# Layer 3 as one pass over x3 with a tap lead of five row groups; layer 2's token factor kept on chip

## The chip, the cores and the metric

The kernel runs on one core of a Trainium2 chip. The metric is device time in microseconds for one execution. The kernel before takes 3590.95 us (median of three runs, 3589.71 to 3592.86). A profile of one execution gives the start and length of every instruction on TensorE (PE), VectorE (DVE), ScalarE (ACT), GpSimd (POOL) and SyncE (SP, which here only issues DMAs).

## The reference, cut to what matters

The input x is a 256 x 256 image with 128 channels, in fp32. Four layers each add something to it, after a group norm over groups of four channels (`_gn`): attention with a triangle bias, a triangle product of 16 channels, a triangle product of 128 channels (layer 2), and a stack of small convolutions (layer 3). The change touches layers 2 and 3.

```python
# layer 2, on z = _gn(x)
zn = layernorm(z)                               # a mean and a root per token
a = sigmoid(zn @ Wga + bga) * (zn @ Wla + bla)
b = sigmoid(zn @ Wgb + bgb) * (zn @ Wlb + blb)
k = einsum('bimc,bmjc->bijc', a, b)
out = sigmoid(zn @ Wgo + bgo) * (layernorm(k) @ Wlo + blo)

# layer 3, on x = _gn(x); c1 is a 1 x 9 convolution with one output channel,
# c2 a product over channels at each token
t = relu(c1(x))
y = concat([x[:, :1], x[:, 1:] + t[:, :-1]], axis=1)
u = relu(c1(y))
z = u + roll(y, 1, axis=1)                      # the last two rows differ
v = relu(c2(z))
p = concat([z[:, :, :1], z[:, :, 1:] + v[:, :, :-1]], axis=2)
r = relu(c2(p))
q = r + roll(p, 1, axis=2)                      # the last two columns differ
```

In layer 3 t and u have a single channel: they are images of 256 x 256 numbers. Since y differs from x by an image that is the same in all channels, c1(y) is c1(x) plus a nine-tap filter of t with the channel sums of the weights, moved down by one row.

## The kernel before, in words

Activations lie in DRAM transposed, 128 channels by 65,536 tokens (`x2T`, `x3T` and others). A stage works through 32 tiles of 2048 tokens (`SC`), a tile of [128 channels, 2048] being eight rows of the image. Every DMA of the stages named here is issued by SP, in program order. The stages with `tc.manual_schedule()` keep the written order on each engine.

*Layer 2, gated products* (L833 to L957, names `p5_...`). Blocks of four tiles. `sums5` forms each token's mean and mean square with matmuls on 32-column strips, `compact5` stores the block's variance to DRAM and reads it back as [128, 64], `root5` and `factor5` take root and reciprocal of that small tile and store it, and `spread5` reads it back broadcast over 128 partitions into the tile `p5_zn`. `normalise5` then multiplies in place, in one DVE instruction of 2048 elements per tile. `product5` makes a gate or a linear product of 1024 tokens (two matmuls) into one of three PSUM buffers; ACT takes the sigmoid of the gate, DVE multiplies the linear product in. The results are stored to `aD` and `bD`, token row first: [128, channel, 512].

*Layer 2, triangle product* (L958 to L1018). Four channels per step are loaded from `aD` and `bD`, transposed and multiplied; K goes to `kD`. *Layer 2, end* (L1022 to L1079) normalises k and z with `broadcast_rows` (L819): four matmuls that spread rows of factors over 128 partitions into two PSUM tiles. For z it uses the tile `rs2`, which POOL loads from DRAM.

*Layer 3, tap pass* (L1115 to L1127). All of x3 is read; one matmul per 512 tokens gives the nine tap sums, which POOL's queue stores to `sD`. *Layer 3, image stage* (L1130 to L1189). The whole images t and u are formed once, and moved by rows through DRAM (`imgD`). Their sum e is added to all channels later. *Layer 3, main loop* (L1196 to L1309, `p9_...`). x3 is read again in groups of eight rows, each tile with the row above it. Per group: ACT scales x into z and q; `finish_z` adds e, spread by `broadcast_rows`, on DVE; `p_half` and `q_half` each run half of a c2 product, with DVE taking relu and sum from PSUM; POOL's `residual` adds p into q; `emit` transposes a finished group back on PE, and ACT copies it out. Two product tiles (`psM`) and two further tiles (`psX`: broadcast and transposes in turn) fill the PSUM.

Of the kernel before, what the change touches and what calls it, by code (L numbers as in the profile page):

```python
# [31 lines left out]
def kernel(ctx: ExitStack, tc: tile.TileContext, a: dict, out: bass.AP):  # L32
# [19 lines left out]

    aD = dram.tile([P, D, 2 * N], F32, name="aD")
    bD = dram.tile([P, D, 2 * N], F32, name="bD")
    vrD = dram.tile([1, T], F32, name="vrD")
    rs2D = dram.tile([1, T], F32, name="rs2D")
# [3 lines left out]
    sD = dram.tile([32, T], F32, name="sD")  # L60
    imgD = dram.tile([4, T], F32, name="imgD")
# [81 lines left out]
    b2 = column("L3_conv_b2")  # L143

# [52 lines left out]
    with tc.tile_pool(name="x0", bufs=1) as xres, tc.tile_pool(name="p0", bufs=3) as sb:  # L197
# [18 lines left out]
        with tc.tile_pool(name="f0", bufs=1) as fsb, tc.tile_pool(name="f0ps", bufs=1, space=PSUM) as ps:  # L216
# [29 lines left out]
            pb2 = ps.tile([P, 6], F32, name="f0_pb2")  # L246
# [4 lines left out]
            nc.vector.tensor_tensor(b2w, b2w, pb2, ALU.add)  # L251
            pt_ = ps.tile([P, NH], F32, name="f0_pt")
# [103 lines left out]
    with tc.tile_pool(name="p2c", bufs=1) as cs:  # L356
# [39 lines left out]
        with tc.tile_pool(name="p2", bufs=2) as sb, tc.tile_pool(name="p2e", bufs=6) as eb, tc.tile_pool(  # L396
# [159 lines left out]
            for j in range(2 * NG + 5):  # L556
# [5 lines left out]
                if not 0 <= out[0] < NG:  # L562
                    out = None
                if half == 0 and nxt:
                    tiles(nxt)
# [266 lines left out]

    rs2_pool = ctx.enter_context(tc.tile_pool(name="rs2", bufs=1))  # L833
    KB = 4
    BT = KB * SC
    with tc.tile_pool(name="p5", bufs=2) as sb, tc.tile_pool(name="p5psX", bufs=1, space=PSUM) as psX, tc.tile_pool(
        name="p5psM", bufs=3, space=PSUM
# [13 lines left out]
        def store_block(dram_row, b, t):  # L851

            by_c = dram_row.rearrange("o (s c t) -> c (o s) t", c=4, t=CK)
            for c in range(4):
                nc.sync.dma_start(
                    by_c[c, b * KB : (b + 1) * KB, :], t[32 * c + b * KB : 32 * c + (b + 1) * KB, :]
                )

        def sums5(b):
            st = psX.tile([P, 2, CK], F32, name="p5_st")  # L860
# [13 lines left out]
            return var  # L874

        def compact5(b, var):
            store_block(vrD, b, var)
            vars_[b] = sb.tile([P, BT // P], F32, name="p5_vc")
            nc.sync.dma_start(
                vars_[b], vrD[:, b * BT : (b + 1) * BT].rearrange("o (p t) -> p (o t)", p=P)  # L880
            )

        def root5(v):
            nc.vector.tensor_scalar(v, v, 0.0, None, ALU.max)
            nc.scalar.activation(v, v, AF.Sqrt, bias=epst)

        def factor5(b):
            v = vars_.pop(b)
            nc.vector.reciprocal(v, v)
            nc.sync.dma_start(  # L890
                rs2D[:, b * BT : (b + 1) * BT].rearrange("o (p t) -> p (o t)", p=P), v
            )

        def spread5(s):
            if s < NSC:
                zns[s] = sb.tile([P, SC], F32, name="p5_zn", bufs=3)
                nc.sync.dma_start(zns[s], rs2D[:, s * SC : (s + 1) * SC].to_broadcast([P, SC]))

        def normalise5(s):
            if s < NSC:  # L900
                nc.vector.scalar_tensor_tensor(zns[s], xs[s], m2, zns[s], ALU.subtract, ALU.mult)  # L901
                del xs[s]
# [14 lines left out]
        var = sums5(0)  # L917
        root5(var)
        fac = sb.tile([P, CK], F32, name="p5_fac", bufs=1)
        nc.vector.reciprocal(fac, var)  # L920
        store_block(rs2D, 0, fac)
        for s in range(2):
            spread5(s)
        normalise5(0)
        for s in range(NSC):
# [5 lines left out]
            for h in range(2):  # L931
                hs = slice(h * H2, (h + 1) * H2)
                for i in range(2):
                    pg = product5(s, 2 * i, h)
                    nc.scalar.activation(ab[i][:, hs], pg, AF.Sigmoid, bias=b2w[:, 2 * i : 2 * i + 1])
                    if (j, h, i) == (2, 1, 0) and b + 1 in vars_:
                        root5(vars_[b + 1])
                    pl = product5(s, 2 * i + 1, h)
                    nc.vector.scalar_tensor_tensor(  # L939
                        ab[i][:, hs], pl, b2w[:, 2 * i + 1 : 2 * i + 2], ab[i][:, hs], ALU.add, ALU.mult  # L940
                    )
                if h == 0:
                    if j < 2:
                        square5((b + 1) * KB + 2 * j + 1)
                    normalise5(s + 1)
                elif j == 2 and b + 1 in vars_:
                    factor5(b + 1)
            spread5(s + 2)
            for dst, t in zip((aD, bD), ab):
                nc.sync.dma_start(  # L950
                    dst[:, :, :].rearrange("p c t -> c p t")[:, 4 * s : 4 * s + 4, :],
                    t.rearrange("c (p t) -> c p t", p=4),
                )
            del zns[s]
            if j == 1 and (b + 1) * KB < NSC:
                compact5(b + 1, sums5(b + 1))
# [3 lines left out]
    rs2 = rs2_pool.tile([P, CK], F32, name="rs2_")  # L960
    for c in range(4):
        nc.gpsimd.dma_start(  # L962
            rs2[32 * c : 32 * c + 32, :], rs2D.rearrange("o (s c t) -> c (o s) t", c=4, t=CK)[c]
        )
    with tc.tile_pool(name="p6", bufs=3) as sb, tc.tile_pool(name="p6s", bufs=1) as ssb, tc.tile_pool(
# [6 lines left out]
        with tc.manual_schedule():  # L972
            quads = {}

            def load6(q):
                if q < D // 4:
                    A = sb.tile([P, 4, 2 * N], F32, name="p6_A")
                    nc.sync.dma_start(A, aD[:, 4 * q : 4 * q + 4, :])
                    B = sb.tile([P, 4, 2 * N], F32, name="p6_B")
                    nc.sync.dma_start(B, bD[:, 4 * q : 4 * q + 4, :])  # L980
# [41 lines left out]
    with tc.tile_pool(name="p7", bufs=2) as sb, tc.tile_pool(name="p7psX", bufs=2, space=PSUM) as psX, tc.tile_pool(  # L1022
# [20 lines left out]
        def normalise_z(s):  # L1043
            rb = broadcast_rows(psX, rs2, s, "p7_rz")
# [51 lines left out]

    w1f = const.tile([P, 32], F32, name="w1f")
# [3 lines left out]
    kcol = const.tile([P, 3], F32, name="kcol")  # L1101
    with tc.tile_pool(name="f3", bufs=1) as sb, tc.tile_pool(name="f3ps", bufs=1, space=PSUM) as ps:
# [6 lines left out]
        pw = ps.tile([P, 1], F32, name="f3_w")  # L1109
        nc.tensor.matmul(pw, lhsT=w2c, rhs=b2, start=True, stop=True)  # L1110
        nc.vector.tensor_scalar(kcol[:, 0:1], b2, -1.0, None, ALU.mult)
        nc.vector.scalar_tensor_tensor(kcol[:, 1:2], pw, -1.0, b2, ALU.mult, ALU.subtract)
        nc.vector.scalar_tensor_tensor(kcol[:, 2:3], b2, 2.0, pw, ALU.mult, ALU.add)

    with tc.tile_pool(name="p8", bufs=4) as sb, tc.tile_pool(name="p8ps", bufs=4, space=PSUM) as ps:  # L1115
        for s in range(NSC):
            ss = slice(s * SC, (s + 1) * SC)
            xt = sb.tile([P, SC], F32, name="p8_x", bufs=6)
            nc.sync.dma_start(xt, x3T[:, ss])
            pp = ps.tile([P, CK], F32, name="p8_s")  # L1120
            for c in range(4):
                nc.tensor.matmul(
                    pp[32 * c : 32 * c + 32, :], lhsT=w1f, rhs=xt[:, c * CK : (c + 1) * CK], start=True, stop=True
                )
            st = sb.tile([P, CK], F32, name="p8_st", bufs=8)
            nc.scalar.activation(st, pp, AF.Identity, bias=s0)
            store_groups(nc.gpsimd, sD, s, st)  # L1127


    with tc.tile_pool(name="img", bufs=1) as sb, tc.tile_pool(name="imgps", bufs=1, space=PSUM) as ps:  # L1130

        def image(k):
            return imgD[k].rearrange("(h w) -> h w", w=N)

        def store(k, t):
            nc.sync.dma_start(image(k).rearrange("(t p) w -> p t w", p=P), t)

        def load_down(t, k, n):

            nc.vector.memset(t[0:32, 0, :], 0.0)  # L1140
            nc.sync.dma_start(t[n:P, 0, :], image(k)[0 : P - n, :])
            nc.sync.dma_start(t[:, 1, :], image(k)[P - n : N - n, :])

        pw = ps.tile([P, TAPS], F32, name="pw")
        nc.tensor.matmul(pw, lhsT=ones, rhs=w1[:, :TAPS], start=True, stop=True)
        wsum = sb.tile([P, TAPS], F32, name="wsum")
        nc.vector.tensor_copy(wsum, pw)
        St = sb.tile([P, TAPS, 2, N], F32, name="St")
        nc.sync.dma_start(
            St.rearrange("p k t w -> p (k t) w"), sD[:TAPS, :].rearrange("k (t p w) -> p (k t) w", p=P, w=N)  # L1150
        )
        acc = sb.tile([P, 2, N], F32, name="acc")
        nc.vector.tensor_copy(acc, St[:, 4, :, :])
        shifts = [(k, max(0, 4 - k), min(N, N + 4 - k)) for k in range(TAPS) if k != 4]
        for k, lo, hi in shifts:
            nc.vector.tensor_tensor(
                acc[:, :, lo:hi], acc[:, :, lo:hi], St[:, k, :, lo + k - 4 : hi + k - 4], ALU.add
            )
        t_ = sb.tile([P, 2, N], F32, name="t_")
        nc.scalar.activation(t_, acc, AF.Relu, bias=b1)  # L1160
        store(0, t_)
        ct = sb.tile([P, 2, N], F32, name="ct")
        nc.vector.tensor_scalar(ct, t_, wsum[:, 4:5], None, ALU.mult)
        for k, lo, hi in shifts:
            nc.vector.scalar_tensor_tensor(
# [326 lines left out]
```

## Time and profile before

The profiled execution took 3590.95 us, and its span, first to last instruction, was 3589.0 us.

| stage | window, us | what it shows |
|---|---|---|
| layer 2 gated products, start | 1926 to 1958 | PE busy 11.5 of 32.0 us |
| layer 2 gated products | 1958 to 2452 | PE busy 492.4 of 494.0, DMA share 0.68 |
| layer 2 triangle product | 2462 to 2750 | PE busy 287.5 of 288.0, DMA share 0.93 |
| layer 2 end | 2780 to 3070 | PE busy 290.0 of 290.0, DMA share 0.85 |
| layer 3 tap pass | 3097 to 3190 | PE busy 49.2 of 93.0, DMA share 1.02 |
| layer 3 image stage | 3196 to 3256 | DVE busy 14.7 of 60.0 |
| layer 3 main loop | 3285 to 3572 | PE busy 287.0 of 287.0, DVE 218.4, DMA share 0.67 |

In the views of the profile a line of the chain of waits gives a start, a length and the work; a line of the timeline adds the number of instructions merged. "L908" is line 908 of the kernel before. A fp32 matmul shows as two PE instructions.

### The profile page before, as it was taken

The numbers are of one execution on the slowest core, as the hardware profiler recorded it, in microseconds if no ns is written. First come the engines' busy times: TensorE is split into PE (matmuls) and PEld (weight loads), VectorE is DVE, ScalarE is ACT, GpSimd is POOL, SyncE is SP. The second block draws the span as 40 slices with busy tenths as digits, with TensorE's granted clock in tenths as the row PEclk, the third lists the DMA queues.
The fourth block names the chain that finished last, engine by engine and source line by source line (L and its number), as shares of the span: only waits on it lengthen the run. The fifth ranks groups of instructions, "written<-read, shape, count | busy, mean of one in ns | idle before, by whom it ended". The sixth has DMA issues, their size and how long they took to land. (4 is left out here: it accounts for less than half of the span.)

```text
span 3589.0 us, 52067 instructions
## 1 busy us (share of the span) xinstructions
PE 3130.1 (87%) x20266; PEld 1649.4 (46%) x20266; DVE 2280.2 (64%) x2522; ACT 1948.9 (54%) x2163; POOL 1631.0 (45%) x852
## 2 busy tenths in 40 slices
PE   4566999999999999955795999998998999636998
PEld 4413555555555555513332444446996333103544
DVE  4625888888888888831695454454555777215776
ACT  3564777777777777632343444443443566414665
POOL 3003777777777777612593000002554444313444
PEclk7887999999999999978897999999998999758999
DMA  9892333333333333278697778667997888675776
GB/s 329 317 344 91 102 119 113 108 114 119 114 110 111 119 117 111 92 296 314 215 329 316 260 259 304 230 245 281 352 351 282 339 336 335 267 284 172 227 226 187
DMA packets 276662, 801.88 MB, mean 223 GB/s; under 512 B 36639, under 2 KB 109612, under 8 KB 221884
## 3 DMA queue, kind: packets, MB, share of 16 engines
q1 hardware_dynamic: 256844, 780.41, 60.9%
q0 software_dynamic: 19568, 18.09, 1.7%
q8 instruction: 162, 2.65, 0.3%
q14 instruction: 88, 0.72, 0.1%
HBM read 504.22 MB, written 294.09 MB: 222 GB/s over the span
## 5 line engine op out<-in xcount | busy, mean ns | idle before, releaser
L468 DVE TENSOR_TENSOR p_e<-p_S,triT 128x1024 f32<-128x1024 f32 x512 | 609.4, 1212 | 144.5 <-PE p_S L458 144.5
L478 POOL TENSOR_TENSOR p_es<-p_e 128x1024 f32<-128x1024 f32 x256 | 603.0, 2366 | 127.5 <-issue 67.5
L476 ACT ACTIVATE p_e<-p_e,mbT 128x1024 f32<-128x1024 f32 x512 | 551.8, 1137 | 63.2 <-DVE p_e L468 61.4
L908 PE MATMUL p_pm<-p_zn,wf 128*128 128x512 f32 x1024 | 443.9, 595 | 15.8 <-DVE p_zn L901 15.8
L443 PE MATMUL p_mm<-p_xn,wf 128*128 128x512 f32 x768 | 409.0, 616 | 8.0 <-POOL p_xn L416 8.0
L416 POOL TENSOR_TENSOR p_xn<-p_xn,p_rs 128x1024 f32<-128x1024 f32 x64 | 153.6, 2400 | 446.4 <-DMA p_rs<-rsD 254.1
L908 PEld LDWEIGHTS p_pm<-p_zn,wf 128*128 128x128 f32 x1024 | 194.8, 191 | 265.1 <-issue 244.5
L458 PE MATMUL p_S<-p_q,p_k 32*128 32x256 f32 x4096 | 295.3, 400 | 5.0 <-DVE p_e L468 5.0
L458 PEld LDWEIGHTS p_S<-p_q,p_k 32*128 32x128 f32 x4096 | 185.8, 184 | 161.5 <-PE p_mm L434 91.7
L1450 PE MATMUL tp_z<-p_B,tp_at 128*128 128x256 f32 x1024 | 250.6, 388 | 0.8 <-DMA p_B<-bD 0.5
L491 PE MATMUL p_o<-p_e,p_v 128*32 128x256 f32 x4096 | 249.2, 384 | 0.0
L1252 POOL TENSOR_TENSOR p_q<-p_q,p_pb 128x2024 f32<-128x2024 f32 x32 | 144.1, 4502 | 220.8 <-DVE p_pb L1246 220.8
L1079 POOL TENSOR_TENSOR p_x<-p_x,p_g 128x2048 f32<-128x2048 f32 x32 | 145.4, 4544 | 182.6 <-DVE p_g L1076 182.6
L1000 POOL TENSOR_TENSOR p_k<-p_k,p_sq 128x512 f32<-128x512 f32 x128 | 162.9, 1273 | 135.8 <-ACT p_sq L998 135.8
L962 POOL DMA_DIRECT2D rs__17975<-rs2D x4 | 2.1, 519 | 466.7 <-DMA rs2D<-p_vc 466.7
L1450 PEld LDWEIGHTS tp_z<-p_B,tp_at 128*128 128x128 f32 x1024 | 185.1, 191 | 23.2 <-DVE tp_at L1441 1.5
L443 PEld LDWEIGHTS p_mm<-p_xn,wf 128*128 128x128 f32 x768 | 126.7, 191 | 113.3 <-issue 90.2
L491 PEld LDWEIGHTS p_o<-p_e,p_v 128*32 128x32 f32 x4096 | 120.5, 110 | 110.0 <-ACT p_g L449 41.5
L999 DVE TENSOR_TENSOR p_k<-tp_z,p_k 128x512 f32<-128x512 f32 x128 | 88.5, 692 | 127.0 <-ACT p_sq L998 127.0
L996 ACT COPY p_K<-tp_z 128x512 f32<-128x512 f32 x128 | 75.1, 586 | 165.4 <-PE tp_z L1450 165.4
L434 PEld LDWEIGHTS p_mm<-wf,p_xn 128*128 128x128 f32 x1024 | 135.5, 193 | 62.9 <-issue 61.9
L939 DVE SCALAR_TENSOR_TENSOR p_b<-p_pm,b2w,p_b 128x1024 f32<-128x1024 f32 x64 | 82.2, 1284 | 125.4 <-PE p_pm L908 111.0
(335 smaller groups left out, 5870.3 us busy)
## 6 DMA issues: line engine op xcount, KB each, us to landing
p_x<-x2T SPq DMA_DIRECT2D x64, 1024.0 KB
p_x<-x1T SPq DMA_DIRECT2D x48, 1024.0 KB
p_x<-x3T SPq DMA_DIRECT2D x31, 1152.0 KB
p_x<-x3T SPq DMA_DIRECT2D x33, 1024.0 KB
p_x<-in_x_dram SPq DMA_DIRECT2D x32, 1024.0 KB
p_x<-xT SPq DMA_DIRECT2D x64, 512.0 KB
p_rs<-rsD SPq DMA_DIRECT2D x64, 512.0 KB
p_rb<-rzD SPq DMA_DIRECT2D x256, 128.0 KB
```

The costliest lines, as they stand in the source:

```text
L416: nc.gpsimd.tensor_tensor(xn, xn, t["rs"], ALU.mult)
L443: nc.tensor.matmul(pm, lhsT=w, rhs=t["xn"][:, cs_], start=True, stop=True)
L458: nc.tensor.matmul(Ss[h // 2][:, h % 2, u, :], lhsT=t["k"][hp, r * N + u * P : r * N + (u + 1) * P], rhs=t["q"][hp, r * N : (r + 1) * N], ...
L468: nc.vector.tensor_tensor(e[:, :, 2 * p : 2 * p + 2, :].rearrange("p u h n -> p h u n"), Ss[p], triT[:, 2 * p : 2 * p + 2, :, :], ALU.add,)
L476: nc.scalar.activation(e[:, u, :, :], e[:, u, :, :], AF.Exp, bias=mbT[:, u, i : i + 1])
L478: nc.gpsimd.tensor_tensor(es, e[:, 0, :, :], e[:, 1, :, :], ALU.add)
L491: nc.tensor.matmul(t["o"][hp, r % 2, :], lhsT=t["v"][:, r * 2 + u, hp], rhs=e[:, u, h, :], start=(u == 0), stop=(u == 1),)
L908: nc.tensor.matmul(pm[:, c, :], lhsT=wf2[:, i, :], rhs=zns[s][:, k * CK : (k + 1) * CK], start=True, stop=True)
L1000: nc.gpsimd.tensor_tensor(k2, k2, sq, ALU.add)
L1079: nc.gpsimd.tensor_tensor(xs[s], xs[s], gt, ALU.add)
L1252: nc.gpsimd.tensor_tensor(q[:, :, 1 : N - 2], q[:, :, 1 : N - 2], pb[:, :, 0 : N - 3], ALU.add)
L1450: nc.tensor.matmul(pz[:, t, :], lhsT=at[:, u, t * P : (t + 1) * P], rhs=Bc[:, u, :], start=(u == 0), stop=(u == 1))
```

## The change: what it does

In layer 2 the token factor no longer goes through DRAM. Root and reciprocal are taken of the whole [128, 512] tile of a block, kept in `rs2[b]`, and `normalise5` spreads it by `broadcast_rows`. The PSUM is shared out anew (`psX` two tiles, `psM` two). `aD` and `bD` become [channel, token] rows. `root5` moves to the first half of a block's third tile and `factor5` behind that half's normalisation.

In layer 3 the tap pass and the image stage go. The main loop loads each group once, forms the taps of the group five ahead, stores them with padded rows, and builds images in blocks of 16 rows: a block is loaded as [128, 9, 40], partition = 16 rows of one of eight 32-column strips with four columns on each side, so that a reduction over the nine tap planes gives c1(x). Moves by one or two rows are products with shifted identity matrices (four of 32 columns in `image_e`); e goes to `eD` in one DMA and comes back in four, as rows for `broadcast_rows`. The tap store's zero columns (`pads`) are written during the attention stage.

```diff
-    aD = dram.tile([P, D, 2 * N], F32, name="aD")
-    bD = dram.tile([P, D, 2 * N], F32, name="bD")
+    aD = rows("aD", D)
+    bD = rows("bD", D)
...
+                if j == 20:
+                    pads = sD_tap[:, 0 : (N + 1) * (N + 8)].rearrange("k (h w) -> k h w", w=N + 8)[:, :, 0:8]
+                    nc.sync.dma_start(pads, zpad.unsqueeze(1).to_broadcast([TAPS, N + 1, 8]))
...
-    with tc.tile_pool(name="p5", bufs=2) as sb, tc.tile_pool(name="p5psX", bufs=1, space=PSUM) as psX, tc.tile_pool(
-        name="p5psM", bufs=3, space=PSUM
+    with tc.tile_pool(name="p5", bufs=2) as sb, tc.tile_pool(name="p5psX", bufs=2, space=PSUM) as psX, tc.tile_pool(
+        name="p5psM", bufs=2, space=PSUM
...
+        def root5(b):
+            nc.scalar.activation(vars_[b], vars_[b], AF.Sqrt, bias=epst)
...
         def factor5(b):
-            v = vars_.pop(b)
-            nc.vector.reciprocal(v, v)
-            nc.sync.dma_start(
-                rs2D[:, b * BT : (b + 1) * BT].rearrange("o (p t) -> p (o t)", p=P), v
-            )
+            nc.vector.reciprocal(rs2[b], vars_.pop(b))
...
         def normalise5(s):
-            if s < NSC:
-                nc.vector.scalar_tensor_tensor(zns[s], xs[s], m2, zns[s], ALU.subtract, ALU.mult)
-                del xs[s]
+            rb = broadcast_rows(psX, rs2[s // KB], s, "p5_rb")
+            zns[s] = sb.tile([P, SC], F32, name="p5_zn")
+            for h in range(2):
+                hs = slice(h * H2, (h + 1) * H2)
+                nc.vector.scalar_tensor_tensor(zns[s][:, hs], xs[s][:, hs], m2, rb[h], ALU.subtract, ALU.mult)
+            del xs[s]
...
-                    if (j, h, i) == (2, 1, 0) and b + 1 in vars_:
-                        root5(vars_[b + 1])
+                    if (j, h, i) == (2, 0, 0) and b + 1 in vars_:
+                        root5(b + 1)
...
                 if h == 0:
                     if j < 2:
                         square5((b + 1) * KB + 2 * j + 1)
-                    normalise5(s + 1)
-                elif j == 2 and b + 1 in vars_:
-                    factor5(b + 1)
+                    if s + 1 < NSC:
+                        normalise5(s + 1)
+                    if b + 1 in vars_:
+                        factor5(b + 1)
...
-                    nc.sync.dma_start(A, aD[:, 4 * q : 4 * q + 4, :])
+                    nc.sync.dma_start(A, aD[4 * q : 4 * q + 4, :].rearrange("c (p t) -> p c t", p=P))
...
+        def taps(x, h0, n):
+            pp = psX.tile([P, 2, CK], F32, name="p9_pp", tag="x")
+            for c in range(n):
+                nc.tensor.matmul(
+                    pp[32 * c : 32 * c + 32, 0, :], lhsT=w1f, rhs=x[:, 2 * c : 2 * c + 2, :], start=True, stop=True
+                )
+            st = sb.tile([P, 2, N], F32, name="p9_st", bufs=3)
+            nc.scalar.activation(
+                st[0 : 32 * n].rearrange("p h w -> p (h w)"), pp[0 : 32 * n, 0, :], AF.Identity, bias=s0[0 : 32 * n]
+            )
+            for c in range(n):
+                h = h0 + 2 * c
+                dst = sD_tap[:, 8 + h * (N + 8) : 8 + (h + 2) * (N + 8)].rearrange("k (h w) -> k h w", w=N + 8)
+                nc.sync.dma_start(dst[:, :, 0:N], st[32 * c : 32 * c + TAPS])
+
+        def load_block(b, r0_, r1_):
+            St = sb.tile([P, TAPS, 40], F32, name="p9_S")
...
+            for q in range(8):
+                at = (b * BR + r0_) * (N + 8) + 32 * q
+                src = sD_shift[:, at : at + (r1_ - r0_) * (N + 8)].rearrange("k (h w) -> h k w", w=N + 8)
+                nc.sync.dma_start(St[BR * q + r0_ : BR * q + r1_], src[:, :, 0:40])
+            return St
+
+        def image_t(b, St, mask):
+            acc = sb.tile([P, 40], F32, name="p9_acc")
+            nc.vector.tensor_reduce(acc, St.rearrange("p k w -> p w k"), AX.X, ALU.add)
+            t = sb.tile([P, 40], F32, name="p9_t")
+            nc.vector.scalar_tensor_tensor(t, acc, b1, mask, ALU.add, ALU.mult)
+            nc.vector.tensor_scalar(t, t, 0.0, None, ALU.max)
...
+            ct = sb.tile([P, 32], F32, name="p9_ct")
+            nc.vector.tensor_scalar(ct, t[:, 0:32], wsum[:, 0:1], None, ALU.mult)
+            for k in range(1, TAPS):
+                nc.vector.scalar_tensor_tensor(
+                    ct, t[:, k : k + 32], wsum[:, k : k + 1], ct, ALU.mult, ALU.add
+                )
...
+        def image_e(b):
+            k, before = blocks[b], blocks.pop(b - 1)
+            pi = psX.tile([P, 2, CK], F32, name="p9_pi", tag="x")
...
+            nc.vector.tensor_tensor(e, ps_u, k["acc"][:, 4:36], ALU.add)
+            nc.vector.tensor_scalar(e, e, b1, 0.0, ALU.add, ALU.max)
...
+                nc.vector.tensor_tensor(e, ps_t, e, ALU.add)
...
         for s in range(NR + 2):
-            load9(s + 3)
+            load9(s + 8)
+            b = (s + 3) // 2 if s % 2 and s + 3 < NR else None
...
                 p_half(s, 0)
                 p_half(s, 1)
                 del xs[s]
+            if b:
+                image_t(b, blocks.pop("S"), inside)
             if s + 1 < NR:
                 finish_z(s + 1)
...
             if s < NR:
                 residual(s)
+            if b:
+                image_e(b)
+            if s + LEAD < NR:
+                taps(xs[s + LEAD], (s + LEAD) * R, 4)
+                if s % 2 == 0:
+                    blocks["S"] = load_block((s + 4) // 2, 0, BR)
             if s > 1:
                 emit(s - 2)
```

Ahead of the loop the changed kernel forms the taps of the last two rows and of groups 0 to 4, and the images of block -1 (two rows of it), block 0 and block 1, in the order taps 0 and 1, image_t and image_e of block 0, taps 2 to 4, image_t of block 1, `finish_z(0)`, image_e of block 1.

## The prediction

> **What bounds the kernel now.** I read the windows by stage first, then the chain of waits, then the timeline of the last stage. By stage (columns: window, its length, busy us of PE, PEld, DVE, ACT, POOL, granted clock, DMA share, GB/s):
>
> ```profile
> 1958.00:2452.00 494.00, 492.44 (x1472) 208.63 (x1472) 241.16 (x181) 221.17 (x183) 2.06 (x4) 0.99 0.68 250
> 2462.00:2750.00 288.00, 287.53 (x1523) 259.79 (x1524) 162.51 (x252) 136.44 (x252) 159.15 (x125) 0.99 0.93 342
> 3097.00:3190.00 93.00, 49.21 (x232) 6.26 (x232) 0.00 (x0) 17.75 (x26) 17.26 (x25) 0.61 1.02 405
> 3196.00:3256.00 60.00, 3.45 (x10) 1.79 (x10) 14.74 (x24) 1.79 (x3) 0.96 (x2) 0.52 0.40 124
> 3285.00:3572.00 287.00, 287.00 (x1167) 145.24 (x1165) 218.35 (x233) 178.37 (x175) 141.42 (x88) 1.00 0.67 214
> ```
>
> TensorE sets the pace of layer 2's gated products (first row), of its triangle products (second, with the DMA at 0.93) and of layer 3's last stage (fifth). The tap pass (third) is a pure x3 read at DMA share 1.0; the image stage (fourth) is latency. The chain has the sizes:
>
> ```profile
> 1945.62 3.37 DVE p_fac L920
> ...
> 1951.57 4.57 DMA p_zn<-rs2D
> ...
> 1995.68 55.13 PE p_pm L908 x128
> 2050.81 7.00 PE p_st L865 x64
> ...
> 3066.24 3.63 PE p_pm L1054 x8
> 3070.95 7.24 PE p_pm L1054 x16
> ...
> 3231.11 8.09 DMA cd<-imgD
> ```
>
> A full-width product instruction costs 55.13/128 = 0.43 us (a 512-column matmul is two of them); 64 instructions on 32-column strips cost only 7.00 us. In L1054's stage a half step of 8 products and one broadcast is 4.70 us: the broadcast costs 4.70 - 8 x 0.43 = 1.25. Layer 3's loop, one row group:
>
> ```profile
> 3409.16 1.14 PE L824 MATMUL p_eb<-p_e,sel 32*128 32x512 f32 x8
> 3410.23 3.70 PE L1238 MATMUL p_pm<-p_pb,w2c 128*128 128x512 f32 x8
> 3413.77 1.91 PE L1275 MATMUL p_pt<-ident,p_q 128*128 128x128 f32 x16
> 3415.51 3.60 PE L1238 MATMUL p_pm<-p_z,w2c 128*128 128x512 f32 x8
> 3419.04 1.14 PE L824 MATMUL p_eb<-p_e,sel 32*128 32x512 f32 x8
> ```
>
> Broadcast to broadcast: 9.88 us, no gap on PE.
>
> **The Trainium skill.** (1) "TensorE: Matmul & The Clock Gate", "What's actually happening": the array runs at half rate once a window of about 3.4 us was idle, and needs a busy window as long to reach full rate. The trace agrees: in the tap pass PE was 53% busy at clock 0.61 and L1122's median was 1061 ns beside 592 for L908. (2) "DMA: Bandwidth & Descriptors", "Anatomy of one DMA": about 2 us fixed, mostly completion. The image stage: store issued 3246.47, dependent load 3248.63, so 2.16. (3) Same page, "Why a DMA increments its semaphore by 16 and not by 1": a copy uses as many engines as the largest number up to 16 dividing both outer sizes. The 127-row load of cd took 8.09 us. (4) Same page, "Specifications": below 512 B a transfer is not at line rate; no run here shows 160 B pieces.
>
> **Layer 2, parts.** *Broadcast on PE*: 31 in-loop broadcasts of 1.25 on the engine that sets the end, +39. The zn traffic leaves (1 of 4 MB per step), but DMA at 0.68 was not the bound, so that gives nothing. *Start*: the factor's trip through DRAM ends (stores 1949.01 to landed zn 1956.17, 7.2) and the first half starts after 1.28 of DVE, not 2.36; the broadcast adds 1.25: -7. *Whole-tile reciprocal*: 3.37 (the p_fac row) seven times in place of 0.54 (L889), on DVE ahead of the next product's eviction, and product buffers fall from three to two. The place is the third tile of a block. Let t = 0 be where PE ends the last linear product of its first half. With two buffers, gates use one and linear products the other. ACT is late by the root and its two table loads (0.73 + 2 x 1.28), so DVE has evicted that product only at 1.7; it normalises two halves (2.56, to 4.3), inverts (3.35, to 7.65) and evicts the next linear product (1.28, to 8.95). PE meanwhile broadcasts (1.2) and makes gate, linear, gate (1.72 each), and at 6.3 wants the linear buffer: it stands 2.7, seven times, +19. Bounds: 0 if the reciprocal falls beside other waits, +25 with it wholly exposed (7 x 3.35, and a little). *aD, bD by rows*: stores become 8 KB runs, the 64 loads of the triangle stage 2 KB runs. Stage one, half 2 KB loads, ran 346 GB/s at share 0.96; the 8 KB stage (2780 to 3070) 323 at 0.85, 380 at full share. So 2 KB loads do about 340, and a four-channel step needs 2.1/0.34 + 1.05/0.367 = 9.0 us of DMA beside 8.98 of PE: +5 (0 to +15). *Pads*: 2313 pieces of 32 B during attention; the skill's rule puts them on 9 engines. SP queues rs and x loads behind; PE was busy throughout that stage and groups are fetched two ahead, so a stop of some 257 pieces per engine mostly hides: +3 (0 to +10). Costed at nothing: POOL's four rs2 loads go (POOL was idle there), zn and pb buffers fall from three to two (their last reader is done one step before the new writer), kcol and wsum move to the set-up (two PE and four DVE instructions of 0.16 to 0.2 us beside stage one's end; about 1 if uncovered). Layer 2 and pads: **+59**.
>
> **Layer 3, start.** Removed: tap pass, image stage, second read. The loop begins with L1232 at 3258.3. After: x loads from 3091.9 as now, 2.45 each (L1122's tiles start 3096.9, 3099.3, 3101.8). In the built order each DMA on SP waits for the one eight before it, so the second group's last tap store waits for the eighth load, 3114.8, and has landed at 3116.5. Sixteen block loads at 0.35 on SP, landed 3123.7; image_t 3.2; image_e 1.7; its store 1.7; four er loads 1.6, issued at 3132. Behind them on SP stand the twelve tap stores of groups 2 to 4 (4.0, landing 1.3), then block 1 (3.0, landing 1.6), and on DVE image_t(1), another 3.2, stands ahead of finish_z(0): **3145, so -113**. These steps lie in series with nothing beside them; 10 us either way.
>
> **Layer 3, loop.** PE gains per row group the taps (8 strip instructions, 7.00/64 x 8 = 0.9, plus 0.3 to switch) and per pair four 32-column products, about 1.0. A pair of groups would be 2 x 9.88 + 2.4 + 1.0 = 23.1. ACT (+0.69 +0.2) and DVE (218/287 busy, +2 per group) stay below that. But the new work is a ring. A block is loaded at the end of the even group, right behind its own tap stores, and image_t reads it in the next group ahead of finish_z on DVE; behind that queue the q evictions and image_e; PE's transposes wait for image_e's PSUM buffer, as psX has two and now feeds pi and pp too. From the taps' eviction (t = 0):
>
> - four tap stores at 0.3 on SP and landing: 2.6; eight block loads at 0.36: 5.5; landed and seen **7.4**. PE has one transpose set left (0.9), then two p products (3.5); their evictions end at 5.9. DVE stands from there to 7.4, with finish_z and both q evictions queued behind it.
> - image_t: a 360-element reduction about 0.5 (L1090's 0.19 for 32 elements, plus length), 11 small ops at 0.24 (L1098's 0.23): 3.2. finish_z 2.36, q 2 x 1.49, e 0.66, waking 0.1: 16.7.
> - then PE-bound: transposes 1.75, p 3.55, broadcast 1.1, q 3.5, taps 1.1, eviction 0.7: 28.4.
> - PE works 2 us of the 7.6 before its transposes; by (1) it goes on at half clock for some us. The trace has no such gap; 0 to 3, taken 1.1.
>
> So **29.5 per pair**, where now 19.76. Fourteen pairs carry blocks (odd s up to 27): 14 x 9.74 = **+136**. Layer 3: +23.
>
> **Sum.** 51 + 5 + 3 - 113 + 136 = +82 on the profiled span of 3589.0: 3671. That execution took 3590.95, 1.95 around the span and the median of the three: **3673**.
>
> **Rivals.** *Image chain hidden*: SP's small copies land before 5.9 and PE never waits for psX: 23.1 a pair, 14 x 3.34 = +47, total -7: 3584; with p5's stall absent 3565. For: PE queues are the only visible bound now, and LEAD is five groups. Against: the lead is spent before the block load, which the order puts one group ahead of its reader. It decides below 19.76 + 54/14 = 23.6 us per pair. *Order alone*: copies in time, no cold clock, 5.9 + 20.9 = 26.8 a pair: 3636; with the reciprocal hidden 3617. *Slow small copies*: 160 B pieces cost (4) a further 3 us and the clock 2: 34 a pair: 3736. *No change at all* would need +81 and -81 to meet: the removed start is certain, the rest is not.
>
> **How the numbers follow.** The forecast's own case (27.5 to 32 a pair, 3645 to 3708) 0.62, order alone 0.18, hidden 0.08, slow copies 0.12. Leaving out the hidden case and most of the slow one's tail gives 3612 to 3730. Against 0.2% (7 us, about what a measurement here can tell from no change): all of the hidden case but 0.01 is faster, 0.07; that 0.01 and 0.02 of the order case, with pairs near 24, are same, 0.03; the rest is slower, 0.90.
>
> **What would show it.** After: a window from the first p_sq to the last p_pm of layer 2's products about 51 longer than now; in the waits, p_pm products waiting for DVE in seven spells near 2.7; the triangle stage at DMA share about 1.0; the last stage's first p product near its group norm plus 55; there, pairs near 29.5 with DVE's reduction waiting for p_S and PE's transposes for DVE, clock under 0.95. Wrong if pairs are near 23, if p_S landed early, or if p5 shows no DVE spells.

## The result, and the profile after

The changed kernel takes 3738.04 us (median of four runs, 3733.76 to 3741.72), beside 3591.9 us (3589.71 to 3603.77) for the kernel before on the same chip: a ratio of 1.040, 95% interval 1.037 to 1.043. It is slower, as forecast, but by 146 us, where the forecast was 82, and just outside the forecast's range.

The windows by stage of the kernel after, cut at the same marks as before (columns: window, length, busy us of PE, PEld, DVE, ACT, POOL, granted clock, DMA share, GB/s):

```profile
1956.00:2504.00 548.00, 532.86 (x1698) 208.28 (x1697) 263.24 (x208) 220.46 (x180) 0.00 (x0) 0.98 0.42 163
2518.00:2808.00 290.00, 283.27 (x1503) 256.48 (x1504) 160.94 (x250) 134.52 (x248) 157.63 (x125) 0.98 0.97 341
3160.00:3213.00 53.00, 12.49 (x62) 4.67 (x54) 11.20 (x32) 6.07 (x9) 0.00 (x0) 0.56 0.38 139
3320.00:3630.00 310.00, 254.14 (x970) 128.63 (x969) 183.66 (x283) 136.50 (x151) 88.08 (x58) 0.82 0.43 130
```

Layer 2's products (first row) are longer, and TensorE has gaps there. The triangle product (second) has kept its length. The tap pass and the image stage have shrunk to one start of some 55 us (third). In the last stage (fourth) no engine is busy throughout any more: PE 254 of 310 us at clock 0.82, where before it was 287.0 of 287.0 at 1.00. By marks in both traces, 62.3 us have been lost up to the end of layer 2's products (1.4 of them ahead of these), nothing in the triangle product (-0.6), about 110 were gained between group norm and the first finish_z, and 193 were lost from there to the end (330.7 to 523.8 us). 62 - 110 + 193 = 145, the difference of the spans, 3734.0 - 3589.0.

The chain of waits at the change of a block in layer 2's products, which has no counterpart before (start, length, work):

```profile
2074.16 2.38 DVE p_zn L897 x2
2076.54 0.60 DVE rs L890
2077.14 2.57 issue
2079.72 1.20 DVE p_a L931
2080.96 10.55 PE p_pm L904 x20
2091.51 1.07 PE p_rb L841 x8
2092.58 13.93 PE p_pm L904 x32
```

The reciprocal (L890, 0.60 and the 2.57 put down to "issue" behind it) stands ahead of the eviction L931, and the products wait. The next 20 products take 10.55 us, 0.53 each, where 32 later ones take 13.93, 0.435 each: 10.55 - 20 x 0.435 = 1.85 us of lower clock follow the gap.

The chain through one pair of row groups in the last stage (the pair begins with ACT's eviction of the taps, p_st):

```profile
3487.28 0.70 ACT p_st L1126
...
3493.93 1.84 DMA p_S<-sD
...
3496.05 0.84 DVE p_acc L1148
3496.91 1.66 DVE p_t L1150
...
3501.28 1.23 DVE p_z L1213
...
3502.55 0.64 PE p_pi L1170 x2
...
3504.47 1.91 PE p_pp L1122 x8
3506.40 0.70 ACT p_st L1126
...
3507.23 3.65 PE p_pt L1256 x16
3510.88 4.32 PE p_pm L1219 x8
3515.20 1.07 PE p_eb L841 x8
3516.27 3.63 PE p_pm L1219 x8
3519.90 1.04 PE p_pp L1122 x8
3520.97 0.70 ACT p_st L1126
```

3520.97 - 3487.28 = 33.7 us. From one reduction L1148 to the next the mean is 33.6 over eleven pairs (3262.55 to 3632.41), where 29.5 was forecast and 23.6 was the break-even. The waits of this stage (engine, tile, line; total us, times, longest):

```profile
PE p_pi L1170 <- DVE p_z L1213: 69.0, 13, 5.3
...
DVE p_acc L1148 <- DMA p_S<-sD: 32.1, 13, 3.0
```

Both look as forecast: VectorE's reduction waits for the block load, 2.5 us a pair, and TensorE waits 5.3 for VectorE. But one line of the chain is odd. L1150 is a small operation, 128 x 40, and takes 1.66 us; at the start of layer 3 the same line takes 0.26. The timeline has the reason beside it (start, length, engine, line):

```profile
3494.04 4.47 POOL L1233 TENSOR_TENSOR p_q<-p_q,p_pb 128x2024 f32<-128x2024 f32 x1 [6.16 <-DVE p_pb L1227]
...
3496.05 0.83 DVE L1148 TENSOR_REDUCE p_acc<-p_S 128x40 f32<-128x360 f32 x1 [2.18 <-DMA p_S<-sD]
3496.91 1.65 DVE L1150 SCALAR_TENSOR_TENSOR p_t<-p_acc,b,p_in 128x40 f32<-128x40 f32 x1
```

GpSimd's add of p to q runs from 3494.04 to 3498.51, and L1150, which reads two SBUF tensors, ends at 3498.56. In the next pair the add ends at 3532.21 and L1150 at 3532.26, although the copies landed later there (reduction at 3530.50, 9.53 us behind the start of the taps' eviction; 8.77 here). So the image may not be waiting for its copies at all. The experiments start there.

### The profile page after: what moved, and what is told of

The parts are those of the page before. It is cut to its first block, busy times and chain, and to the rows that moved or that the text cites. A ratio compares the mean times of both kernels' runs of the same rounds, so it can differ in the third digit from the quotient of the medians.

```text
span 3734.0 us, 53373 instructions
## 1 busy us (share of the span) xinstructions
PE 3252.3 (87%) x20652; PEld 1708.6 (46%) x20652; DVE 2373.3 (64%) x2782; ACT 1961.0 (53%) x2194; POOL 1608.6 (43%) x826
## 4 chain that ended last, share of the span: by engine, by line
PE 38%; DMA 8%; DVE 5%; issue 3%; SPq 2%; ACT 2%; POOL 1%; DVEq 0%; ACTq 0%; POOLq 0%
PE p_pm L904 10%; PE p_pm L1038 6%; PE tp_z L1483 6%; PE p_pm L1219 4%; PE tp_a L1472 2%; DMA abD<-p_ab 2%; PE p_pt L1256 1%; PE p_pg L791 1%; DMA p_x<-x1T 1%; DMA x2T<-p_x 1%; SPq L1142 1%; PE p_st L874 1%; PE p_pp L1122 1%; PE p_rz L841 1%; PE p_rk L841 1%
## 5 line engine op out<-in xcount | busy, mean ns | idle before, releaser
L904 PE MATMUL p_pm<-p_zn,wf 128*128 128x512 f32 x1024 | 464.6, 611 | 16.5 <-DVE p_a L931 15.1
L1227 DVE SCALAR_TENSOR_TENSOR p_pb<-p_pm,kcol,p_z 128x1020 f32<-128x1020 f32 x64 | 81.9, 1280 | 149.0 <-PE p_pm L1219 149.0
L931 DVE SCALAR_TENSOR_TENSOR p_b<-p_pm,b2w,p_b 128x1024 f32<-128x1024 f32 x64 | 82.2, 1284 | 145.7 <-PE p_pm L904 127.9
```

The costliest lines, as they stand in the source:

```text
L904: nc.tensor.matmul(pm[:, c, :], lhsT=wf2[:, i, :], rhs=zns[s][:, k * CK : (k + 1) * CK], start=True, stop=True)
```

## The experiments

**One part alone.** Layer 3 changed, layer 2 as before:

```diff
-    aD = rows("aD", D)                 # and bD, p5, rs2, loads of p6: all as in the kernel before
+    aD = dram.tile([P, D, 2 * N], F32, name="aD")
```

> The layer 3 part of the change alone: layer 2's gated products and triangle stage are the ones of the kernel before (factors by DMA broadcast, short reciprocal, a and b stored by triangle tile), layer 3 is the changed one. In the marks of the two profiles layer 2 gave +62 us up to the last p5 product and nothing after it. If the two parts don't touch each other: 3738 - 62 = 3676 us, with the loop of layer 3 unchanged at 33.5 to 34.5 us a pair of row groups. If the layout of a and b or the freed rs2 space had helped a later stage, the saving is smaller, 40 to 55 us: 3683 to 3698.

Measured: 3675.66 us, ratio 1.021 (1.018 to 1.025). This is the time expected if the parts are independent, and the pair stays at 33.6 us. Layer 2's part costs 62 us and layer 3's 79 to 84, and they don't touch each other.

**Layer 2's stall.** The whole-tile reciprocal cut into four, one behind each of four evictions:

```diff
-            nc.vector.reciprocal(rs2[b], vars_.pop(b))
+            nc.vector.reciprocal(rs2[b][:, ks], vars_[b][:, ks])   # ks: 128 of 512 columns
```

> Changed kernel with the reciprocal of layer 2's factor (128x512, seven times) cut into four of 128x128, one behind each of four product evictions, in place of one whole at the end of an h = 0 half; it is complete one eviction before the factor's first use. The seven stalls of TensorE (2.25 us each and 1.95 us of half clock behind it, 4.2 in all) should go: p5's block period from 71.3 to about 67.1 us (62.1 and four broadcasts of 1.25), 3738 - 7 x 4.2 = 3709. If VectorE has no slack at those places and the quarters delay evictions all the same: 3725 to 3738. If the stall isn't the reciprocal's: 3738.

Measured: 3712.59 us, 25 less than the changed kernel (ratio to before 1.032, 1.028 to 1.035). The chain of this kernel over one block:

```profile
2065.10 7.06 PE p_pm L907 x16
2072.16 1.07 PE p_rb L841 x8
2073.24 13.96 PE p_pm L907 x32
...
2132.33 7.06 PE p_pm L907 x16
2139.40 1.07 PE p_rb L841 x8
```

No gap is left, and the block's period is 2139.40 - 2072.16 = 67.24 us; with the whole reciprocal it was 71.33, before the change 62.13. So a stall cost 4.09 us, 1.85 of it the lower clock and 2.24 the gap, and four broadcasts cost 5.1, 1.28 each. One stall of the seven was cheaper: the block behind the third gap took 69.64 us, and the granted clock after that gap stayed at 1.00, where it was 0.50 for some 3.4 us after the second. From the first product to the end of the last, the quarters saved 26.8 us (532.5 for 559.3), which is 7 x 2.24 + 6 x 1.85. At the start 6 us were gained: the first product comes 25.2 us behind the stage's first load (1928.79 to 1954.02), before 31.2 (1927.43 to 1958.64). 31 broadcasts at 1.28 and the seven stalls make 39.7 + 26.8 - 6 = 60.5; the stage lost 60.9.

**The wait for the copies taken away.** Taps six groups ahead, the block loaded a whole iteration before its use, all else in the same order:

```diff
-    LEAD = 5
+    LEAD = 6
...
-                if s % 2 == 0:
-                    blocks["S"] = load_block((s + 4) // 2, 0, BR)
+                if s % 2:
+                    blocks["S"] = load_block((s + 5) // 2, 0, BR)
```

> Changed kernel with the taps six row groups ahead instead of five, and the image block loaded at the end of the odd iteration, a whole iteration before the one that reduces it; the order of the image's operations on VectorE and TensorE is kept. Theory A (the ring goes through order and clock: image operations in front of finish_z on VectorE, the row moves and taps behind it in the psX ring, TensorE at half clock after the gap; of the copies only the wait of the reduction shows): the wait of the reduction on p_S, 32.1 us over 13 pairs, goes, 2.5 us a pair, and 0 to 0.5 of clock with it: 31 to 31.5 us a pair, 3738 - 14 x 2.5 to 3.0 = 3696 to 3703. Theory B (the small copies bind: all 8.8 us from the taps eviction to the reduction lie on the ring, as in the rival 'slow small copies'): the pair falls to 25 to 28, 3610 to 3655. Theory C (TensorE's clock alone sets it): 3730 to 3738.

Measured: 3733.64 us, 1.038 (1.035 to 1.042), and a pair of 33.5 us instead of 33.6. The wait of the reduction on p_S is gone from the loop, and nothing was gained: neither theory A's 2.5 us nor theory B's 6 to 9. The time lies in the range of theory C (TensorE's clock alone), but the timeline shows something that none of the three had:

```profile
3488.63 0.83 DVE L1148 TENSOR_REDUCE p_acc<-p_S 128x40 f32<-128x360 f32 x1
3488.89 4.47 POOL L1233 TENSOR_TENSOR p_q<-p_q,p_pb 128x2024 f32<-128x2024 f32 x1 [6.17 <-DVE p_pb L1227]
...
3489.50 3.92 DVE L1150 SCALAR_TENSOR_TENSOR p_t<-p_acc,b,p_in 128x40 f32<-128x40 f32 x1
```

The reduction now starts right behind the p evictions, and L1150 lasts 3.92 us in place of 1.65. It again ends with GpSimd's add (3493.36 and 3493.42). What was a wait for a DMA has become a long instruction. The mean of L1150 in this stage went from 1.35 to 3.91 us.

**That add left out.** If the add is what holds L1150, leaving it out must free it:

```diff
             q, pb = qs[s], pbs[s]
+            if s % 2:
+                nc.gpsimd.tensor_copy(q[:, :, 0:1], pb[:, :, N - 1 : N])
+                return
             nc.gpsimd.tensor_tensor(q[:, :, 1 : N - 2], q[:, :, 1 : N - 2], pb[:, :, 0 : N - 3], ALU.add)
```

> The kernel of lead6, with GpSimd's add of p to q left out in the odd iterations (a 128x8 copy stands for the three adds, so part of the residual is missing from the output). In lead6 the first image operation that reads two SBUF tensors (p_t, L1150) lasts 3.9 us instead of 0.26, and ends when the 4.47 us add of GpSimd ends. Theory L (VectorE and GpSimd lock each other out, and that took the place of the wait for the copies): p_t falls to 0.26, and each pair loses 3.65 us, from 33.9 to 30.3, or to 27 to 29 where the shorter gap also leaves TensorE at a higher clock: 3734 - 14 x 3.65 to 6.5 = 3643 to 3683. Theory M (p_t waits for something else, a buffer or a semaphore): 3728 to 3738, p_t still near 3.9.

Measured: 3649.72 us, 1.015 (1.012 to 1.017), 84 us less than with the add; the pair is 27.5 us. The timeline:

```profile
3419.40 0.83 DVE L1148 TENSOR_REDUCE p_acc<-p_S 128x40 f32<-128x360 f32 x1
...
3420.27 0.26 DVE L1150 SCALAR_TENSOR_TENSOR p_t<-p_acc,b,p_in 128x40 f32<-128x40 f32 x1
```

L1150 takes 0.26. Of the 6.0 us a pair, 3.65 are the lock itself; TensorE's gap ahead of the row moves fell from 5.3 to 1.65 us, and with it some of the half clock (the taps behind it took 1.06, in the changed kernel 1.94; the transposes still 3.40). The Trainium skill has the mechanism, "SBUF — State Buffer", section "SBUF: two separate sides": VectorE and GpSimd share one port pair, "an exclusive lock, not a bandwidth split", taken for the whole instruction by whichever comes first, among others by a VectorE operation with two SBUF inputs. These traces agree: 1.65 and 3.92 us under a 4.47 us add, 0.26 without it. They also show what isn't held up: the reduction L1148 (one SBUF input) took 0.83 us under the add as elsewhere.

**TensorE's clock.** The products of the second q half repeated while TensorE waits for finish_z, three times and four times over:

```diff
-            for c in range(2):
+            for c in [c for c in range(2) for _ in range(times)]:
```

> Changed kernel with the two products of the second q half computed three times over into the same tile in the odd iterations: 4 more 512-column products (4 x 0.86 = 3.4 us at full clock) on TensorE, in the 5.3 us in which its queue waits for finish_z; results and order are kept. If half clock after that gap is on the ring (theory A: row moves +0.9, taps +0.9, transposes +1.9, p +1.0 = 4.7 a pair), the granted clock of the loop rises from 0.82 to 0.95 or more and the pair falls to 29 to 30.5: 3738 - 14 x 3.5 to 5 = 3668 to 3689. If the clock isn't on the path, 3733 to 3745; if the repeats don't lift the clock they run at half, 6.9 us, and add 1.5 a pair: 3760.

> As fill, with the two products of the second q half computed four times instead of three (6 more products, 5.2 us at full clock) in the odd iterations of the changed kernel. In fill the repeats ended 2.5 us before finish_z, and TensorE was at half clock again behind it: row moves, taps (1.91) and transposes (3.5) lasted as long as before, and the pair fell by 1 us only. Here the gap is filled. Theory A (half clock behind the gap is 3.5 to 4.6 us of the pair): taps after finish_z last 1.06, transposes 1.97, the pair falls to 29.5 to 31, 3738 - 14 x 3 to 4.5 = 3675 to 3696. If the clock isn't worth that: 3715 to 3725 as fill. If the repeats outlast the gap they add up to 1 us a pair.

Measured: 3723.21 us (1.035, 1.032 to 1.039) with three, 3700.27 us (1.029, 1.028 to 1.031) with four; pairs of 31.8 and 29.9 us. The first misses theory A's range; the second is 4 us above it, with its pair inside. Three times left a gap of 1.9 to 2.5 us, and that was enough in most pairs: over twelve of them the transposes behind it took 3.3 to 3.65 us eleven times, the taps 1.93 five times and 1.06 to 1.37 in the others. Four times left 0.15 to 0.7 us of the gap, and there the taps took 1.06 and the transposes 2.35. The same window of the changed kernel, and then of the one with four:

```profile
3260.00:3560.00 300.00, 244.16 (x928) 123.97 (x928) 180.17 (x279) 128.71 (x144) 87.36 (x54) 0.83 0.45 137
3260.00:3560.00 300.00, 286.05 (x1161) 132.99 (x1160) 200.90 (x311) 144.48 (x160) 97.09 (x60) 1.00 0.49 152
```

The clock went from 0.83 to 1.00, although TensorE has been given 5.2 us more work in each pair. Half clock was worth 3.7 us a pair in the steady stretch and 38 us on the whole, while both the lock and the copies are still there.

**The order turned round.** The image's VectorE operations behind the q evictions, its row moves behind the p products of the next iteration:

```diff
-            if b:
-                image_t(b, blocks.pop("S"), inside)
+            if s % 2 == 0 and 2 <= s < NR - 2:
+                image_e((s + 2) // 2)
             if s + 1 < NR:
                 finish_z(s + 1)
...
             if b:
-                image_e(b)
+                image_t(b, blocks.pop("S"), inside)
```

> Changed kernel with LEAD 5 and the same loads, but the image's VectorE operations (image_t) issued after the q evictions of the odd iteration instead of ahead of finish_z, and the row moves (image_e) issued after the p products of the next iteration. Nothing is left out. Theory A (order and clock): finish_z, and so eb, q, taps and the next pair no longer wait for copies or image, TensorE is busy nearly without gaps at full clock, and the pair falls to the TensorE sum 23.1 plus up to 2: 23.5 to 25 us, 3738 - 14 x 9 to 10.5 = 3591 to 3612. Theory B (copies bind): the reduction still waits for p_S and the pair stays over 28, above 3655. Theory C (half clock comes from TensorE's evictions by VectorE, not from the image chain): clock stays near 0.82 in the loop, pair 28 to 30, 3655 to 3685.

Measured: 3718.46 us, 1.034 (1.030 to 1.037), a pair of 32.5 us. The time lies in theory B's range, but the reduction no longer waits for p_S at all, and the clock is 0.88 in the stage; no theory had the cause right. The timeline:

```profile
3468.17 4.52 DVE L1177 TENSOR_SCALAR p_e<-p_e,b 128x32 f32<-128x32 f32 x1
3468.21 4.45 POOL L1233 TENSOR_TENSOR p_q<-p_q,p_pb 128x2024 f32<-128x2024 f32 x1 [7.06 <-DVE p_e L1176]
...
3472.97 2.08 PE L841 MATMUL p_eb<-p_er,sel 32*128 32x512 f32 x4 [5.28 <-DVE p_e L1183]
3474.98 6.47 PE L1219 MATMUL p_pm<-p_pb,w2c 128*128 128x512 f32 x8
```

The lock has found another victim. The image operations now run when GpSimd is idle, but the row moves' L1177 (128 x 32, one SBUF input) falls under the add: 4.52 us, where it takes 0.24. (Its record starts 0.04 us ahead of the add's, so the records don't tell which of the two was first; it ends with the add, 3472.69 and 3472.66.) TensorE waits 5.28 for it, and its next products run at half clock (6.47 for eight, 3.60 at full).

**The locked operation removed.** The last three image operations become two that each read one PSUM and one SBUF operand:

```diff
-            nc.vector.tensor_tensor(e, ps_u, k["acc"][:, 4:36], ALU.add)
-            nc.vector.tensor_scalar(e, e, b1, 0.0, ALU.add, ALU.max)
+            nc.vector.scalar_tensor_tensor(e, ps_u, b1, k["acc"][:, 4:36], ALU.add, ALU.add)
...
-                nc.vector.tensor_tensor(e, ps_t, e, ALU.add)
+                nc.vector.scalar_tensor_tensor(e, e, 0.0, ps_t, ALU.max, ALU.add)
```

> The kernel of late, with the image's last three VectorE operations joined to two that each read one PSUM and one SBUF operand: e = (u + b1) + acc, then e = max(e, 0) + t. The operation that lasted 4.53 us under GpSimd's add (p_e, L1177, SBUF to SBUF) is gone; values are the same up to the order of two additions. Theory L (lock): the 4.3 us go from each pair, and the half clock after that gap (4 broadcasts 1.0, q products 1.7 to 2.8) with them: from 32.9 to 25 to 26.5, towards TensorE's 23.1 at full clock; 3718 - 14 x 6.5 to 8 = 3606 to 3627. Theory M (the wait was for the row moves or the ring): the pair stays at 31 to 33, 3690 to 3718.

Measured: 3632.59 us, 1.011 (1.008 to 1.013), a pair of 25.5 us, in theory L's range; the time is 6 us above it. That is 86 us from three 0.2 us instructions made into two. The timeline:

```profile
3438.19 0.24 DVE L1176 SCALAR_TENSOR_TENSOR p_e<-p_pi,b,p_acc 128x32 f32<-128x32 f32 x1
3438.45 4.48 POOL L1233 TENSOR_TENSOR p_q<-p_q,p_pb 128x2024 f32<-128x2024 f32 x1 [7.04 <-DVE p_e L1176]
3438.47 0.19 DVE L1183 SCALAR_TENSOR_TENSOR p_e<-p_e,p_pi 128x32 f32<-128x32 f32 x1
```

L1183 runs under the add in 0.19 us: an operation with one operand in PSUM is not held.

With layer 2 as before, the same layer 3:

> The same layer 3 as in late_port, with layer 2 as in the kernel before. If the two parts stay independent as the layer 3 part alone showed (3675.7 against 3738), 62 us less than late_port: 3544 to 3565, which is 27 to 48 us below the kernel before. If late_port stays near 3700 this one gives 3640.

Measured: 3571.9 us, 0.994 (0.992 to 0.996) of the kernel before, 61 less than late_port. The parts stay independent; the figure is 7 us above what was expected, as late_port's was 6 above.

**A version without gaps.** LEAD 6, image operations in the even iteration behind q, row moves in the odd one behind the taps:

> Layer 2 of the changed kernel; taps six groups ahead, block loaded at the end of the odd iteration, image operations after the q evictions of the even one, row moves after the taps of the odd one, last image operations joined as in late_port. Against late_port it takes the row moves and broadcasts away from behind the p products, where a gap of 0.8 us and 1.7 us of half clock in the q products were left in each pair of 26.4. Expected: 24 to 25 us a pair, near TensorE's 23.1: 3632.6 - 14 x 1.4 to 2.4 = 3599 to 3613. If the row moves now hold the transposes up in the ring: 25.5 to 27, 3620 to 3640.

Measured: 3594.18 us, 0.9995 (0.9985 to 1.0004), 5 us below the range expected. A pair takes 23.14 us (3255.21 to 3509.78, eleven pairs), which is the sum of TensorE's work that the prediction gave for a hidden image chain, 23.1. The window of the stage:

```profile
3260.00:3560.00 300.00, 296.92 (x1328) 143.51 (x1328) 237.74 (x380) 182.81 (x205) 126.65 (x78) 0.99 0.59 178
```

TensorE is busy 297 of 300 us at clock 0.99. And this kernel, with layer 2's loss of 62 us, ties with the kernel before, near the point where the prediction put break-even, pairs of 23.6.

Last, this layer 3 with layer 2 as before, the first x3 loads spread out, and the last block's maximum on ScalarE:

> late6_port with layer 2 of the kernel before, and two edits at the ends of layer 3: only x3 groups 0 and 1 are loaded ahead of the first tap stores, groups 2 to 5 behind those stores and 6, 7 behind the first block loads (in the layer 3 of late_port the first tap stores waited 18.7 us behind eight 1 MB loads); and the last block's maximum is on ScalarE, away from GpSimd's add. From 3571.9: 14 x 1.4 to 2.4 = 20 to 34 less for the loop, 9 to 13 less for the start, 3 to 5 less at the end: 3520 to 3540, 0.980 to 0.985 of the kernel before. If the loads only move the wait to groups 2 to 4: 3532 to 3552.

Measured: 3533.78 us (3532.78 to 3537.24), 0.983 (0.982 to 0.984) of the kernel before: 63 us faster than it, and 204 faster than the changed kernel. The loop gave what was expected (23.14 a pair). The load order gave 2 us only: the tap stores no longer wait for eight loads, but the block loads behind them now wait for groups 2 to 5, the case that the expectation named last. The maximum on ScalarE gained nothing, where 3 to 5 us were expected: in this order it already ran behind GpSimd's add in late6_port (0.18 us).

## Why the prediction was right or wrong

- *Direction and place*: right. Slower, through a ring in layer 3's loop, with p5's cost beside it, and the two parts add up as summed.
- *Broadcast on PE, +39*: right; 1.28 us each over a block, 39.7 in all. *Start of layer 2, -7*: -6.
- *Whole-tile reciprocal, +19*: the mechanism was right, the size too small. TensorE stood 2.24 us (2.7 forecast), but the half clock behind the gap, 1.85 us after six of the seven, was left out: 26.8 in all. The prediction priced half clock in layer 3 and not here. This is 8 of the 10 us by which layer 2's products exceed the forecast; broadcasts and start are the rest.
- *aD, bD by rows, +5*: -0.6 measured. The DMA share went to 0.97, not over 1, so the loads stayed behind TensorE's work. *Pads, +3*: at most 1.4.
- *Start of layer 3, -113*: about -110.
- *Loop, 29.5 a pair*: wrong, 33.6, and 14 x 4.1 = 57 us of the 65 missed. The failing step is "landed and seen 7.4 ... DVE stands from there", with "image_t: ... 3.2" put behind it. It took the block load to be what releases the image. In fact GpSimd's add, released by the same p evictions that the prediction ended at 5.9, keeps the port from 6.1 to 10.6, and the image's second operation can't end before that: 10.6 us from the taps' stored eviction to the end of L1150 (3487.97 to 3498.56), where the step gives 7.4 + 0.5 + 0.24 = 8.1. So the copies, for which the step has 7.4 and which took 8.1 here, were hidden, as the rival "order alone" had said of them, but behind another wait.
- *How much of that is the add*: without it the second operation would have ended at 8.1 + 0.84 + 0.26 = 9.2, an estimate from this trace. So of the 2.5 us by which the step fell short, the add puts 1.4 on top; the other 1.1 come from copies 0.7 later and a reduction 0.3 longer than forecast, and lie under the add. The prediction speaks of POOL's work only where loads leave its queue; it never set the 4.5 us add beside VectorE's new SBUF operations. That lock was in the skill and not in the prediction. The kernel before has no SBUF-to-SBUF operation of VectorE in this loop, so this stage of its trace could not show one being held.
- *Half clock, 1.1*: too small. Transposes took 3.65 for 1.75 and the first p products 4.32 for 3.55, so 2.7 a pair on this path. Not all of it is clock: in fill4, at full clock, the same transposes took 2.35. The six filling products of fill4 recovered 3.7 a pair. 2.5 us for the later end of the image's second operation, 0.3 for the other small image operations and 2.7 - 1.1 = 1.6 for transposes and products make 4.4, beside the 4.2 by which the pair shown exceeds the forecast. The prediction's point (1) asked for an idle window of about 3.4 us and read the tap pass as agreeing. It agrees only in part: from 3128 to 3140 us of the kernel before, TensorE's longest gap was 1.9 us and the granted clock was 0.50. That was a sign that short gaps cost clock too.
- *Rival "order alone", 26.8 a pair*: copies in time, as it says, but neither lock nor half clock. By its own steps it is 5.9 + 28.4 - 7.4 = 26.9.
- *Rival "slow small copies", 34 a pair, 3736*: the number was met, the reason was not. Hiding the copies moved the time by 4 us. A forecast that had rested on it would have been right by accident.
- *Rival "hidden", 23.1 a pair, 3584*: not what the change did, but late6_port showed that the pair stands once nothing blocks VectorE and TensorE has no gap (23.14). The whole, 3594, is 10 us longer, as layer 2's products were.
- *What would show it*: the signs named (reduction waiting for p_S, TensorE waiting for VectorE, clock under 0.95) were all there. They don't tell the copy wait from the lock, since a wait ahead of a held instruction only shortens the hold.

That the lock holds the image, and that the half clock lies on the ring, is shown by the add left out, the joined operations and the filled gap. That nothing else of size is left, once order and copies are changed too, is shown by the pair of 23.14. How the 4.1 us divide is read from the chain: in this kernel the lock and the copies lie side by side, and no run took the lock alone away from it. How much of the half clock comes from the gap alone, and how much from the tiny row moves that follow it, wasn't tried separately.

## What to carry to other kernels

When small VectorE operations are put into a loop, set each one beside what GpSimd runs at that time, not only beside what it waits for: a long duration of a tiny instruction is a wait that no view of waits lists, and reading one operand from PSUM, or a place where GpSimd is idle, removes it. Before crediting the removal of a wait, ask what would release the instruction next; here 2.5 us of DMA wait stood in front of a hold that ended at the same time either way. And price each gap on TensorE with the half clock behind it, which was nearly as large as the gap in layer 2 (1.85 beside 2.24 us, after six gaps of seven).

## What the runs showed of the hardware that was not expected

- A 128 x 32 VectorE operation took 4.52 us, and a 128 x 40 one 3.92, under a 4.47 us GpSimd add; 0.24 and 0.26 without. Held were one with two SBUF inputs and one with a single SBUF input and output (L1177). Not held were a reduction from SBUF (0.83 in both cases) and operations with one PSUM operand (L1183 of late_port 0.19; in the changed kernel the two of finish_z 2.35 together, with the add of the even iteration beside them). GpSimd's add kept its 4.5 us throughout.
- Gaps of 1.6 to 2.2 us on TensorE were followed by half clock: 1.64 us in lead6_noadd (sixteen transposes 3.4 to 3.65 us in the steady stretch, beside 2.35 in fill4), 1.9 in fill (eight tap products 1.93 in five pairs of twelve, beside 1.06), 2.2 in layer 2 (after six gaps of seven). The Trainium skill ("TensorE: Matmul & The Clock Gate", "What's actually happening") speaks of an idle window of about 3.4 us; here shorter gaps did it, though not every time. Whether the narrow products around some of these gaps have a part in it isn't shown.
- 5.2 us of useless products per pair made the kernel 38 us faster.
